# When the layer-0 experts' first loads count as ready: a change to the planner's costs in a two-layer mixture-of-experts kernel

## The chip, the cores and the metric

The kernel runs on one core of a Trainium2 chip. The metric is the device time of one execution in microseconds (us). The engines are named as in the profile: PE is TensorE (PEld its weight loads), DVE is VectorE, ACT is ScalarE, POOL is GpSimd and SP is SyncE, which issues most DMAs. L833 stands for line 833 of the kernel's source.

## The reference

Four sequences (B = 4) of 1024 tokens with 128 channels go through two layers. Each layer normalizes and modulates its input, adds a gated attention, normalizes and modulates again, and adds a gated mixture of experts. Cut to what matters here, the mixture of experts of layer 0:

```python
def _L0_ffn_ref(x, router_w, expert_w1, expert_b1, expert_w2, expert_b2):
    router_probs = softmax(einsum('bnc,ec->bne', x, router_w))
    expert_weights, expert_idx = top_k(router_probs, 2)
    expert_weights = expert_weights / (expert_weights.sum(-1, keepdims=True) + 1e-09)
    h = gelu(einsum('bnc,efc->bnef', x, expert_w1) + expert_b1, approximate=False)
    out_all = einsum('bnef,ecf->bnec', h, expert_w2) + expert_b2
    out_k = take_along_axis(out_all, expert_idx[..., None], axis=2)
    return (out_k * expert_weights[..., None]).sum(axis=2)

# layer 0
h = layernorm(x) * (1 + ca) + sa
x = x + ga * attention0(h)            # one head, causal, 128 channels
h = layernorm(x) * (1 + cb) + sb
x = x + gb * _L0_ffn_ref(h, ...)      # 8 experts, 512 hidden channels, 2 of 8 per token
# layer 1: the same frame; its attention has 16 heads of 8 channels, a second attention that keeps
# the 204 largest weights of each row, and a feed-forward part; its mixture of experts has a capacity
```

## The kernel before

All activations x are kept in on-chip memory, as [128 tokens, batch, 8 row tiles, 128 channels]. The work runs in these stages: the attention of layer 0 with the routing of its experts beside it; the experts of layer 0; the start of layer 1's attention; the long loop of layer 1's attention; the experts of layer 1.

**The experts of layer 0 go through memory outside the core.** For each batch b, `sent_out` normalizes x (the statistics on DVE, L482 and L486; the power -1/2 on POOL, L489; the shift on DVE, L492; the normalizing activations on ACT, L494), modulates the result on DVE (L746, L747), transposes it on PE (`ptf`, L755), computes the router's products (`pl`, L533), and then routes: a series of small DVE operations (`r_mx` to `into`, L545 to L630) with two matmuls `pp` (L595, L596) that count the tokens in front of each token. The result `into` says to which place of which expert's buffer each token's row goes. Sixteen indirect DMAs, issued by POOL (L785), write the rows to the buffer `sent`. Two batches share one buffer: batches 0 and 1 form the first half, batches 2 and 3 the second.

`worked_on(q)` then runs the experts on half q. It loads blocks of 384 and 256 rows of each expert from `sent` (`got`, L820, issued by SP), 16 blocks in all, and each load waits for all 32 indexed writes of its half. For every block PE transposes the rows (`ptg`, L833), DVE copies them out (`hs`, L835), PE makes the hidden rows (`ph`, L865) and ACT applies the activation (`hid`, L869), PE multiplies again (`py`, L850), DVE adds the bias (`y`, L855), and SP stores `y` to `done` (L856). Blocks follow each other in a pipeline: the transposes of block i stand in front of the hidden rows of block i-1 and the products of block i-2.

`fetched(b)` takes the results back: for each of the 8 row tiles POOL issues two indirect gathers from `done` (`ys`, L976); two row tiles later ACT scales one result (L988) and DVE adds the other, applies the gate and adds to x (L989, L990, L991). `begin(0)` starts layer 1's attention for batch 0: normalization, two elementwise operations on POOL (`h_`, L504), transposes on PE (L1257), projections, and two tensors `near` that are written out and loaded back by `project` in another layout (`kg`, `qg`, L1315). The first maxima of the attention (`pm` on PE, L1688; `mxh` on DVE, L1692) are the Part `early`.

**What sets the order.** Each engine executes its instructions in the order in which the program issues them. That order is made by a planner that runs while the program is written. Work is cut into pieces (generators that yield at the end of each piece), and a `Part` wraps a generator. Every yield names the costs of its piece as pairs of engine and microseconds; `spend` adds them to the planner's own clocks, `free["P"]`, `free["A"]`, `free["D"]` and `free["G"]` for PE, ACT, DVE and POOL, and returns the time at which the piece's result is there, which becomes the part's `ready`. An entry `("-", us)` is time on no engine. `fits` lets a piece go when its `ready` and the engines named in the yield's first string are not too far ahead of `free["P"]`. `drain` takes the first part of a list that fits; if none does, it moves `free["P"]` on by 0.2:

```python
            if e == "-":
                t += us
            else:
                ...
                t = free[e] = max(free[e], t) + us
            ...
            t += 0.06
```

These costs are the planner's; they only set the order. Two drains matter here:

```python
    drain([sends0[2], sends0[3], works0[0]])
    ...
                    drain([gets0[0], begins[0], projects[0, 0], early, gets0[1], works0[1]])
```

In the first, the routing of batches 2 and 3 (`sends0`) is planned beside the experts of the first half (`works0[0]`). In the second, the taking back of batches 0 and 1 (`gets0`), the start of layer 1 and its first maxima are planned beside the experts of the second half (`works0[1]`). After it the planner sets all its clocks to their maximum, and the attention loop places its side work by their differences.

Of the kernel before, what the change touches and what calls it, by code (L numbers as in the profile page):

```python
# [21 lines left out]
G = 4  # L22
# [26 lines left out]
def kernel(ctx: ExitStack, tc: tile.TileContext, a: dict, out: bass.AP):  # L49
# [456 lines left out]
    def rows_of(r, n=NT):  # L506
        return r.unsqueeze(1).to_broadcast([P, n, C])
# [291 lines left out]
    def behind(reads, writes, reason):  # L799
        for to in writes:  # L800
            tc.add_manual_dep(
                reads.ins, to.name,
                mybir.DependencyInfo(mybir.DependencyClass.Sync, mybir.DependencyReason.DATA),
                reason=reason,
            )

    def worked_on(q, w1, w2, b2r, fp):

        n = PLACES[0]
        units = [(e, i0, m) for e in range(E) for i0, m in RUNS]  # L810
        most = max(m for _, m in RUNS)
        gots, hss, hids = {}, {}, {}

        def at(u, t):
            e, i0, m = u
            return t[0][q][e * n + i0 * P : e * n + (i0 + m) * P].rearrange("(m p) c -> p m c", p=P)

        def load(u):
            gots[u] = fp.tile([P, most, C], F32, tag="got", bufs=4, name=f"got0{q}")
            got = nc.sync.dma_start(out=gots[u][:, : u[2]], in_=at(u, sent))  # L820
            behind(got, sent_by[0, q], "a place that any of them may have filled")

        load(units[0])
        load(units[1])
        yield "", ("-", 2.5)
        for i in range(len(units) + 2):
            if i < len(units):
                u = units[i]
                if i + 2 < len(units):
                    load(units[i + 2])  # L830
                pt = ps.tile([P, u[2], P], F32, tag="ms", name=f"ptg0{q}")
                for k in range(u[2]):
                    nc.tensor.transpose(pt[:, k, :], gots[u][:, k, :], ident)  # L833
                hss[u] = fp.tile([P, most * P], F32, tag="hs", name=f"hs0{q}")
                nc.vector.tensor_copy(hss[u][:, : u[2] * P], pt.rearrange("c m p -> c (m p)"))  # L835
                yield "A!", ("P", 0.25 * u[2]), ("D", 0.15 + u[2] * 0.14)
            if 1 <= i <= len(units):
                u = units[i - 1]
                hids[u] = fp.tile([P, NK, most * P], F32, tag="hid", name=f"hid0{q}")
                for k0 in range(0, NK, 2):  # L840
                    up(0, u[0], k0, hss[u][:, : u[2] * P], hids[u], AF.Gelu, w1)
                    us = u[2] * P / 512.0
                    yield "A!" if k0 == 0 else "!", ("P", 1.8 * us), ("A", 0.45 + 0.75 * us)
            if i >= 2:
                u = units[i - 2]
                e, _, m = u
                py = ps.tile([P, m, C], F32, tag="ms", name=f"py0{q}")
                for r in range(m):
                    for k in range(NK):
                        nc.tensor.matmul(  # L850
                            py[:, r, :], lhsT=hids[u][:, k, r * P : (r + 1) * P],
                            rhs=w2[:, e, k, :], start=(k == 0), stop=(k == NK - 1),
                        )
                y = fp.tile([P, most, C], F32, tag="y", name=f"y0{q}", bufs=3)
                nc.vector.tensor_tensor(y[:, :m], py, rows_of(b2r[:, e, :], m), ALU.add)  # L855
                nc.sync.dma_start(out=at(u, done), in_=y[:, :m])  # L856
                yield "!", ("P", 0.9 * m), ("D", 0.15 + 0.13 * m)
        yield "", ("-", 3.0)

    def up(l, e, k0, hs, hid, act, w1):  # L860

        n = hs.shape[1]
        ph = psb.tile([P, 2, 512], F32, tag="big", name=f"ph{l}{e}")
        for k in range(k0, k0 + 2):
            nc.tensor.matmul(  # L865
                ph[:, k - k0, :n], lhsT=w1[:, e, k * P : (k + 1) * P], rhs=hs, start=True, stop=True
            )
        for k in range(k0, k0 + 2):
            nc.scalar.activation(  # L869
                hid[:, k, :n], ph[:, k - k0, :n], act, bias=b1[l][:, e * NK + k : e * NK + k + 1]  # L870
            )
# [336 lines left out]
    for n in range(len(tiles) + 2):  # L1208
# [11 lines left out]
    drain(beside[len(begins0) + len(sends0) :] + sends0[:2])  # L1220
    works0 = [
        Part(worked_on(q, w1_0, w2_0, b2r0, f0), after=[sends0[2 * q + 1]])
        for q in range(2)
    ]
# [850 lines left out]
```

## Time and profile before

| | us |
|---|---|
| Median of 6 runs | 1937.03 |
| Lowest and highest of them | 1924.09, 1944.73 |
| The profiled execution | 1930.58 |
| Its span (first to last instruction) | 1928.8 |
| PE busy | 1747.8 (91% of the span) |
| DVE busy | 1279.6 (66%) |
| ACT busy | 1143.4 (59%) |
| POOL busy | 472.9 (25%) |

The mean granted clock of TensorE in the profiled execution was 0.949 of full speed. Matmuls are pipelined and their ends are modelled, so a busy PE is not a PE at its peak. In rows of the order of time, the first number is the start in us from the span's start, the second the time that the instruction (or the row of instructions of one kind) took; "x8" counts the instructions; the brackets at the end give how long the engine stood idle before and what released it. SPq is SyncE's queue of DMA issues; the time of such a row is the issue, not the transfer.

The stages that the change touches lie early in the span: the routing of layer 0 from about 70 us on, the experts' first half from 198 to 281 us, the second half with the start of layer 1 from 284 to 415 us. The loop of layer 1's attention starts at about 418 us.

### The profile page before, as it was taken

What the parts mean: (1) busy time and instruction counts of PE and PEld (TensorE: products, weight loads), DVE (VectorE), ACT (ScalarE), POOL (GpSimd) and SP (SyncE); (2) the same over time, 40 slices, a digit from 0 to 9 for tenths busy, and PEclk for the clock granted to TensorE, in tenths of its full rate; (3) what the DMA queues carried; (4) which work ended last, traced back from release to release, by engine and by line L of the source; (5) the groups of instructions that cost most, each with busy time, mean ns of one, the idle gap of its engine ahead of it and who ended that gap; (6) DMA issues with size and microseconds to landing.
All of it is one profiled execution on the core that took longest, in us unless ns stands there. A gap on an engine that the chain in (4) does not pass through costs nothing.

```text
span 1928.8 us, 33736 instructions
## 1 busy us (share of the span) xinstructions
PE 1747.8 (91%) x12781; PEld 882.0 (46%) x12781; DVE 1279.6 (66%) x3198; ACT 1143.4 (59%) x2317; POOL 472.9 (25%) x515
## 2 busy tenths in 40 slices
PE   6886899899999999998999999999999989999884
PEld 4655777552333434432344435234343423444674
DVE  5666414547877796577886676787776589882453
ACT  3533435246867765686773568778456887565543
POOL 1043356123011020103123110222410122431352
PEclk9988899999999999998998999999999989998998
DMA  8511233110000000000000000000000000002243
GB/s 299 173 34 42 84 95 87 50 44 25 11 18 12 7 2 7 1 7 6 23 12 9 7 1 7 1 17 18 18 5 5 5 6 5 19 1 73 75 116 94
DMA packets 82908, 73.24 MB, mean 38 GB/s; under 512 B 13560, under 2 KB 72521, under 8 KB 82737
## 3 DMA queue, kind: packets, MB, share of 16 engines
q1 hardware_dynamic: 74880, 57.06, 9.9%
q0 software_dynamic: 7424, 13.54, 2.4%
q8 instruction: 103, 1.69, 0.4%
q14 instruction: 69, 0.56, 0.1%
q10 hardware_dynamic: 432, 0.40, 0.1%
HBM read 35.92 MB, written 36.75 MB: 38 GB/s over the span
## 4 chain that ended last, share of the span: by engine, by line
PE 68%; DVE 13%; ACT 10%; issue 4%; DMA 3%; POOL 2%; SPq 0%; DVEq 0%; POOLq 0%; ACTq 0%
PE pw L1704 27%; PE pav L1726 12%; PE ph L865 4%; PE py L850 3%; PE po L1491 3%; DVE mxh L1692 3%; PE pm L1688 2%; ACT prT L1708 2%; DVE nm L1464 2%; ACT junk L1558 2%; ACT exq L1467 2%; PE pf L1805 2%; PE pk L1459 2%; PE ph L1792 1%; PE pscr L1131 1%
## 5 line engine op out<-in xcount | busy, mean ns | idle before, releaser
L1692 DVE TENSOR_REDUCE mxh<-pm 128x2 f32<-128x1024 f32 x512 | 620.5, 1220 | 212.0 <-PE pm L1688 209.3
L1704 PE MATMUL pw<-qa,kg 32*128 32x512 f32 x2048 | 708.5, 662 | 43.6 <-ACT prT L1708 32.4
L1708 ACT ACTIVATE prT<-pw 128x512 f32<-128x512 f32 x1024 | 556.5, 595 | 311.7 <-PE pm L1688 190.6
L1688 PE MATMUL pm<-kg,qg 32*128 32x512 f32 x2048 | 597.8, 663 | 3.3 <-DMA qg<-qk 2.2
L1704 PEld LDWEIGHTS pw<-qa,kg 32*128 32x128 f32 x2048 | 218.6, 189 | 311.1 <-issue 146.0
L1726 PE MATMUL pav<-prT,v_more 128*9 128x256 f32 x3584 | 288.6, 395 | 0.0
L1726 PEld LDWEIGHTS pav<-prT,v_more 128*9 128x9 f32 x3584 | 53.8, 89 | 356.2 <-issue 355.4
L869 ACT ACTIVATE hid<-ph,b 128x160 f32<-128x160 f32 (+2 forms) x256 | 100.1, 457 | 164.5 <-PE ph L865 164.2
L1558 ACT ACTIVATE junk<-exq,now 128x1024 bf16<-128x1024 f32 x160 | 184.7, 1155 | 9.2 <-DVE now L1585 8.5
L1688 PEld LDWEIGHTS pm<-kg,qg 32*128 32x128 f32 x2048 | 161.1, 189 | 13.5 <-DVE mxh L1692 6.0
L1641 POOL TENSOR_TENSOR exq<-exq,lfq 128x512 f32<-128x512 f32 x64 | 80.9, 1285 | 330.9 <-DVE lfq L1639 323.2
L865 PE MATMUL ph<-hs,w 128*128 128x160 f32 (+2 forms) x512 | 125.7, 388 | 16.2 <-DVE go L904 10.0
L865 PEld LDWEIGHTS ph<-hs,w 128*128 128x128 f32 x512 | 86.5, 201 | 40.1 <-DVE mxh L1692 7.9
L976 POOL DMA_INDIRECT ys<-done,outof x64 | 64.3, 1004 | 135.0 <-DMA qg<-qk 65.1
L785 POOL DMA_INDIRECT sent<-xns,into x64 | 62.7, 980 | 77.3 <-DVE into L625 30.9
L850 PEld LDWEIGHTS py<-w,hid 128*128 128x128 f32 x640 | 76.8, 195 | 7.1 <-issue 3.0
L850 PE MATMUL py<-w,hid 128*128 128x128 f32 x640 | 78.2, 279 | 0.0
L489 POOL TENSOR_TENSOR rs_l<-rs_l,mhalf 128x8 f32<-128x8 f32 (+1 forms) x10 | 14.0, 1404 | 225.8 <-DVE rs_l L488 225.8
L1491 PE MATMUL po<-sV,exT 128*128 128x129 f32 x512 | 65.6, 281 | 2.0 <-ACT exT L1487 1.1
L1491 PEld LDWEIGHTS po<-sV,exT 128*128 128x128 f32 x512 | 59.6, 191 | 15.7 <-issue 5.9
L1139 ACT ACTIVATE pr<-pscr,nm 128x128 f32<-128x128 f32 (+7 forms) x32 | 23.6, 739 | 69.3 <-DVE nm L1136 37.2
L1467 ACT ACTIVATE exq<-pk,nms 128x1024 f32<-128x1024 f32 x32 | 35.6, 1112 | 45.2 <-DVE nms L1466 45.0
(540 smaller groups left out, 2289.0 us busy)
## 6 DMA issues: line engine op xcount, KB each, us to landing
w<-in_w_dram SPq DMA_DIRECT2D x32, 256.0 KB
sent<-zero SPq DMA_DIRECT2D x2, 2560.0 KB
done<-zero SPq DMA_DIRECT2D x4, 1024.0 KB
qk<-near SPq DMA_DIRECT2D x8, 512.0 KB
ys<-done SPq DMA_DIRECT2D x16, 256.0 KB
got<-sent SPq DMA_DIRECT2D x16, 192.0 KB
done<-y SPq DMA_DIRECT2D x16, 192.0 KB
sent<-nowhere SPq DMA_DIRECT2D x4, 645.0 KB
```

The costliest lines, as they stand in the source:

```text
L850: nc.tensor.matmul(py[:, r, :], lhsT=hids[u][:, k, r * P : (r + 1) * P], rhs=w2[:, e, k, :], start=(k == 0), stop=(k == NK - 1),)
L865: nc.tensor.matmul(ph[:, k - k0, :n], lhsT=w1[:, e, k * P : (k + 1) * P], rhs=hs, start=True, stop=True)
L869: nc.scalar.activation(hid[:, k, :n], ph[:, k - k0, :n], act, bias=b1[l][:, e * NK + k : e * NK + k + 1])
L1467: nc.scalar.activation(ex, pk, AF.Exp, bias=nms, scale=rscale, accum_out=z)
L1491: nc.tensor.matmul(po, lhsT=exT[:, k, :], rhs=sVs[b % 2][:, k, :], start=(k == 0), stop=(k == NT - 1),)
L1558: nc.scalar.activation(junk, ex, AF.Sign, bias=now[:, i, 0:1], scale=-1.0, accum_out=now[:, i, 1:2],)
L1641: nc.gpsimd.tensor_tensor(ex[:, half(h)], ex[:, half(h)], lf[:, half(h)], ALU.subtract)
L1688: nc.tensor.matmul(pm[:, jj, :], lhsT=qg[js, t0 : t0 + P], rhs=kg[js, half(kh)], start=True, stop=True,)
L1692: nc.vector.tensor_reduce(mx[:, q, j0 : j0 + 2, kh], pm, AX.X, ALU.max)
L1704: nc.tensor.matmul(pw, lhsT=need(b, g, h)[1][js, k * P : (k + 1) * P], rhs=qas[b, g, h][js, :], start=True, stop=True,)
L1708: nc.scalar.activation(prs[b, g, h, k][:, j, :], pw, AF.Exp)
L1726: nc.tensor.matmul(to, lhsT=v, rhs=pr[:, j, cs], start=(k == 0), stop=((k, part) == (NT - 1, 1)),)
```

## The change

One yield of `worked_on` is changed. It stands behind the first two loads of a half, and names what the part waits for before its first transposes:

```diff
         load(units[0])
         load(units[1])
-        yield "", ("-", 2.5)
+        yield "", ("G", 0.0), ("-", 3.2)
         for i in range(len(units) + 2):
```

Before, the part counts as ready 2.5 us after time 0 of the planner, because a part that has not run yet starts from a `ready` of 0. After, the entry `("G", 0.0)` first takes the time to the planner's clock of POOL, `free["G"]`, to which the indexed writes that were issued so far have been added, and 3.2 us follow. Both halves of the experts go through this yield. No instruction of the chip is added, removed or altered by it, and no wait; the order of the instructions in the engines' queues can change.

## The prediction

> **What bounds the kernel now.** I read the page first, then the waits of the stretch that the edit touches, then that stretch in order of time.
>
> ```profile
> span 1928.8 us, 33736 instructions
> PE 1747.8 (91%) x12781; PEld 882.0 (46%) x12781; DVE 1279.6 (66%) x3198; ACT 1143.4 (59%) x2317; POOL 472.9 (25%) x515
> ```
>
> TensorE (PE) is busy 91% of the span, so a reordering can win only PE's idle stretches. The waits from 90 to 520 us give those of the layer-0 experts (groups by line: total, times, longest):
>
> ```profile
> PE ptg L833 <- DMA got<-sent: 19.1, 2, 15.3
> DVE hs L835 <- PE ptg L833: 19.7, 3, 13.0
> ```
>
> 19.1 us in two waits: the first expert transpose of each half waits for its loaded rows. In order of time, the first:
>
> ```profile
> 185.15 0.86 DVE L482 BATCH_NORM_STATS2 st_f<-x 128x6 f32<-128x128 f32 x4
> 193.21 0.97 POOL L785 DMA_INDIRECT sent<-xns,into  x1 [0.30 <-issue]
> 195.60 3.72 SPq L820 DMA_DIRECT2D got<-sent  x5
> 198.06 1.58 PE L833 MATMUL ptg<-ident,got 128*128 128x128 f32 x5 [15.28 <-DMA got<-sent]
> 200.01 0.18 DVE L566 TENSOR_SCALAR r_chosen<-r_left 128x64 f32<-128x64 f32 x1
> ```
>
> GpSimd (POOL) ends the 16 indexed writes of batch 1 at 194.18, SyncE issues the load at 195.60, PE starts at 198.06. VectorE (DVE) stood behind `hs` meanwhile and resumes batch 2's routing only at 200.01. The second:
>
> ```profile
> 284.04 1.08 POOL L976 DMA_INDIRECT ys<-done,outof  x1 [13.46 <-DMA done<-y]
> 284.74 1.30 PE L833 MATMUL ptg<-ident,got 128*128 128x128 f32 x5 [3.79 <-DMA got<-sent]
> 285.65 0.89 DVE L835 COPY hs<-ptg 128x384 f32<-128x384 f32 x2 [4.23 <-PE ptg L833]
> 286.26 4.66 PE L865 MATMUL ph<-hs,w 128*128 128x384 f32 x8 [0.22 <-DVE hs L835]
> ...
> 304.56 0.35 DVE L989 SCALAR_TENSOR_TENSOR ys<-ys,both 128x128 f32<-128x128 f32 x1 [1.75 <-DMA ys<-done,outof]
> 307.71 0.35 DVE L989 SCALAR_TENSOR_TENSOR ys<-ys,both 128x128 f32<-128x128 f32 x1 [2.15 <-ACT ys L988]
> 318.79 4.59 POOL L504 TENSOR_TENSOR h__3028<-h__3028,brow 128x512 f32<-128x512 f32 x4
> 322.30 0.66 PE L1257 MATMUL pt<-ident,h__3028 128*128 128x128 f32 x4 [2.44 <-POOL h__3028 L504]
> 347.97 1.35 SPq L1315 DMA_DIRECT2D kg<-qk  x4
> 352.81 1.55 PE L1688 MATMUL pm<-kg,qg 32*128 32x512 f32 x8 [2.21 <-DMA qg<-qk]
> ```
>
> Here `hs` of the second half goes at once; batch 0's gathers start at 284.04 and their last result is weighed (L989) at 307.71.
>
> **What the edit does to the order.** It adds and removes no instruction and no wait. It changes when the planner takes `worked_on` as ready, so only the order in the queues. I worked that order out from the costs in the source; no time below comes from them. When the first half's loads are issued, the planner's clocks stand at P 193.9, D 198.9, G 204.1. Ready was 0.06 + 2.5 = 2.6, at once. It becomes 204.1 + 0.06 + 3.2 + 0.06 = 207.4. Until then these go in front of the first transposes: the rest of batch 2's routing up to `into` (two matmuls `pp`), batch 3's last statistics, its power on POOL and its first four normalizing activations.
>
> The same function runs for the second half, which the edit's wording doesn't speak of. There P stands at 295.1 and the first piece of batch 0's gathers has just set G to 297.2, so ready is 297.2 + 3.3 = 300.5. Each gather piece is two gathers of 2.1, and a piece goes when G is at most P + 1.0. So gather pieces 0, 1 and 2 fit before P reaches 300.1; piece 2 holds the weighing of row tile 0 (one ACT, three DVE operations). It now stands ahead of the first `hs`, row tile 1 ahead of the second, row tile 2 ahead of `hs` of the third block, row tiles 6 and 7 ahead of the second activation of the third block's hidden rows. DVE and ACT run in order, so the experts now wait for gathers.
>
> **First half: -0.4 us.** The 15.28 us stays, since the writes that end at 194.18 and the load behind them are not moved. What moves into it is DVE work that no PE instruction waited for. Is it done in time? Batch 3's power now follows the writes on POOL: 194.6 to 196.25 (1.68 as at 213.45); its shift on DVE 196.6, six routing operations of 0.8 together (as from 211.79): 197.6, before 198.96, when `hs` could go. Cover 1.4 us; without it each us costs a us. From 204.75 on PE is busy without a break apart from a few tenths, so only `pp` (0.44 us, at 205.94) leaves the path. Bounds: -1.0, if the 0.54 us that batch 3's `pp` waits at 235.21 goes too, and +0.3, if the power slips by its whole length.
>
> **Second half, step by step.**
> 1. Row tile 0 needs the gathers at 284.04 and 285.43. A gather that DVE waited for was released 3.4 us after its start (301.16 to 304.56). So DVE has it at 288.8, three operations (0.35 + 0.29 + 0.29 with gaps: 1.1) to 289.9, `hs` 0.55, hidden matmuls at 290.2 instead of 286.26: +4.0. Bounds: the page's median from issue to landing is 2.6 (+3.1), the longest 4.8 (+5.4).
> 2. Row tile 7 still ends at 308.7: 16 gathers at 1.3. But the activation that frees a `big` buffer for the fourth block's second hidden pair is now behind it (307.7 to 308.75). PE reaches that pair at 305.5 and idles 3.3. The fifth block's PE work starts 7.3 late.
> 3. Batch 0's layer-1 normalization starts when row tile 7 is in x, as before. Its power starts 0.2 later. Then two gathers of batch 1 (2.6) now stand between the multiply and the add of `h_` on POOL (the 4.59 row was unbroken): PE's transposes at 322.30 go to 324.95, +2.65. PE reaches them at some 322.5, so step 2 is absorbed in this wait. But one block less is done by then (`ptg`, `ph`, `py`: 0.4 + 2.75 + 1.95 = 5.1): 7.75 behind.
> 4. The `kg`/`qg` loads come 4.84 us before the first `pm` (347.97 to 352.81), and follow SyncE's store of `y` of block 6. In front of `pm` stood 4.6 us of PE work after that block; now nothing. Counting PE's pieces by the rows from 338.05 on (1.3 + 1.1 + 1.3 + 1.9 + 1.8 + 1.7 + 0.3 + 1.8 + 2.7 = 13.9) from 340.65, block 6 ends at 354.5, the store is issued at 355.3, the loads at 355.75, `pm` goes at 360.6: +7.8, with an idle of 6.1 instead of 2.21.
> 5. Three pieces (2.9 us: `ptg`, `ph`) are still to do that were done before: 10.7 behind at the end of this stretch (before: 414.8).
>
> From there the planner sets all its clocks to their maximum, and the last pieces stand in the same relative order and distances; the order of the attention loop is the old one, only later. Nothing gives the loss back.
>
> **Sum.** -0.4 + 10.7 = +10.3 us. The profiled execution took 1930.58 (span 1928.8 and 1.8 around it): 1940.9. The runs shown have their median at 1937.03, 6.4 above it, so I name 1937.0 + 10.3 = 1947.3. Bounds of the sum: if the idle before `pm` is covered (-3.9) and gathers land by the median (-0.9), +5.5; with the longest landing (+1.4) and 4.8 us of half clock in the new idle, unabsorbed, +16.5.
>
> **The clock.** After the 3.16 us idle at 127.5, PE's granted clock was 0.51 from 130 to 140 and its rows lost 4.8 us; after 2.44 us at 319.9 sixteen 128-wide matmuls took 3.43 instead of 1.95. So I price the new 3.3 us idle as a cold start of 1.5 to 4.8, 2.4 of it absorbed by step 3. The Trainium skill (TensorE: Matmul & The Clock Gate, "What's actually happening") says that it takes about 3.4 us of idling to halve the clock. By that rule this idle is just too short and step 2 costs no cold start; the shorter idle above went cold all the same, and by the row up to 2.4 us would be added.
>
> **Rivals.**
> - *Neutral, or no move*: steps 3 and 4 hidden, or the planner's G below the writes' end so that nothing moves: 0 to +4, 1937 to 1941. For: PE is 91% busy and the tail is identical. Against: the in-order chain from the gathers to `hs`.
> - *Slower by over 1%*: the clock. If each of the three longer idles (before 290.2, 308.85, 360.6) costs the 4.8 us of the worst case, with what 284.74 (2.5) and 352.81 (2.1) already pay taken off: 14.4 - 4.6 = +9.8 on top, 1957.1. It decides once `ph` and `pm` run at half speed some 10 us after each. For: the 130 to 140 slice. Against: 286.26 recovered within 5 us.
> - *Faster*: both expert waits vanish, 15.28 + 3.79 = -19.1: 1918. For: they are PE's longest. Against: the writes and the last `done<-y` set them, and neither moves.
>
> **How the numbers follow.** Forecast 0.55, neutral 0.11, slower rival 0.27, faster 0.07. This kernel's runs tell about 1% (19.4 us) from no change. Faster by over 1%: most of the faster case, 0.05. Slower: the clock case and a small upper tail of the forecast, 0.30. Within 1%: 0.65. The range leaves out the faster case and the far end of the clock case, and allows for the spread of the runs' median: 1930 to 1964.
>
> **What would show it.** Right: `ptg` still at 198 after some 15 us; `r_chosen` near 186 and batch 2's writes from about 198 instead of 215; `ys` L989 before the first `hs` of the second half, with `hs` near 290; POOL's L504 broken by gathers; about 6 us of idle before the first `pm`; the attention loop some 10 us later. Wrong: a shorter first wait, `hs` before `ys`, or a main loop in another order.

## The result, and the profile after

The changed kernel takes 1952.33 us (median of 20 runs, 1932.23 to 1966.73), the kernel before 1932.9 (46 runs). The ratio is 1.0092, with a 95% interval of 1.0069 to 1.0114: some 17.8 us lost, between 13 and 22. It leaves out the five slowest of the 20 executions (1961.99 us and more); the two medians are 19.4 us apart. The forecast had +10.3. The profiled execution of the changed kernel took 1951.97 us.

From its page:

```profile
PE 1762.1 (90%) x12781; PEld 892.5 (46%) x12781; DVE 1281.9 (66%) x3198; ACT 1145.0 (59%) x2317; POOL 473.0 (24%) x515
```

TensorE executes the same 12781 matmuls, but is busy 14.3 us longer with them (1762.1 against 1747.8). Time in which a matmul waits is idle, not busy, in these rows, so part of the loss lies in slower matmuls: between the first `pm` and the first `pw` behind it TensorE is busy 68.07 us instead of 58.09. The waits from 90 to 520 us (total, times, longest):

```profile
PE ptg L833 <- DMA got<-sent: 12.2, 2, 8.3
...
DVE hs L835 <- PE ptg L833: 5.7, 3, 2.6
...
PE pm L1688 <- DMA qg<-qk: 6.5, 1, 6.5
...
PE ph L865 <- DVE hs L835: 5.2, 2, 5.0
```

The expert waits have gone from 19.1 to 12.2 us (the rest of the first stands before `pp` now), and the time is longer all the same. Two other waits have grown: the first `pm` waits 6.5 us for its loads (2.2 before), and `ph` waits 5.0 us for `hs` (0.2 before). The first half in order of time (start, length, instruction, idle before it and its releaser):

```profile
187.87 0.18 DVE L566 TENSOR_SCALAR r_chosen<-r_left 128x64 f32<-128x64 f32 x1
188.19 0.66 PE L595 MATMUL pp<-r_chosen,earlier 128*128 128x64 f32 x2 [3.46 <-DVE r_chosen L566]
...
191.21 0.69 PE L596 MATMUL pp<-r_before,ones 128*128 128x64 f32 x2 [2.36 <-DVE r_before L589]
...
195.16 0.97 POOL L785 DMA_INDIRECT sent<-xns,into  x1 [0.30 <-issue]
197.55 3.91 SPq L820 DMA_DIRECT2D got<-sent  x5
...
199.33 1.04 POOL L785 DMA_INDIRECT sent<-xns,into  x1 [1.50 <-ACT xns L494]
200.20 1.30 PE L833 MATMUL ptg<-ident,got 128*128 128x128 f32 x5 [8.30 <-DMA got<-sent]
```

Two `pp` now cut the old 15.28 us wait into 3.46, 2.36 and 8.30: 14.1 us of idle and the two `pp`. The transposes still start 5.0 us after the start of batch 1's last write (195.16 to 200.20; 4.85 before). Batch 2's writes begin at 199.33 instead of 215.32, and nothing on TensorE had been waiting for them. The second half:

```profile
285.56 1.08 POOL L976 DMA_INDIRECT ys<-done,outof  x1 [27.77 <-DMA done<-y]
...
286.33 1.30 PE L833 MATMUL ptg<-ident,got 128*128 128x128 f32 x5 [3.86 <-DMA got<-sent]
...
291.09 0.35 DVE L989 SCALAR_TENSOR_TENSOR ys<-ys,both 128x128 f32<-128x128 f32 x1 [8.16 <-DMA ys<-done,outof]
...
292.01 0.55 DVE L835 COPY hs<-ptg 128x384 f32<-128x384 f32 x1
...
292.62 5.49 PE L865 MATMUL ph<-hs,w 128*128 128x384 f32 x8 [4.98 <-DVE hs L835]
...
307.91 0.35 DVE L989 SCALAR_TENSOR_TENSOR ys<-ys,both 128x128 f32<-128x128 f32 x1 [0.68 <-DMA ys<-done,outof]
...
319.00 2.32 POOL L504 TENSOR_TENSOR h__2981<-h__2981,brow 128x512 f32<-128x512 f32 x2
...
323.94 2.32 POOL L504 TENSOR_TENSOR h__2981<-h__2981,brow 128x512 f32<-128x512 f32 x2
...
325.18 0.66 PE L1257 MATMUL pt<-ident,h__2981 128*128 128x128 f32 x4 [1.97 <-POOL h__2981 L504]
...
361.64 2.58 PE L1688 MATMUL pm<-kg,qg 32*128 32x512 f32 x8 [6.52 <-DMA qg<-qk]
...
368.12 3.35 PE L1688 MATMUL pm<-kg,qg 32*128 32x512 f32 x8
...
377.60 3.48 PE L850 MATMUL py<-w,hid 128*128 128x128 f32 x16
...
381.02 1.14 PE L1688 MATMUL pm<-kg,qg 32*128 32x512 f32 x8
```

`hs` stands behind the weighing of row tile 0 (L989), the add and the multiply of L504 are apart, and `pm` starts at 361.64: the chain that the prediction had drawn. The last lines show what it had not: eight matmuls of `pm` take 2.58 us at 361.64 and 3.35 at 368.12, and eight of the same form take 1.14 at 381.02. The granted clock, which this text calls half or cold at 0.50 and warm at 1.00, stands behind the four busy times in each row of the windows (window, its length, PE, PEld, DVE, ACT, POOL, clock, DMA share, GB/s):

```profile
358.00:360.00 2.00, 0.00 (x0) 0.00 (x0) 0.00 (x0) 0.00 (x0) 0.00 (x0) 1.00 0.27 88
360.00:362.00 2.00, 0.35 (x2) 0.39 (x3) 0.00 (x0) 0.00 (x0) 0.00 (x0) 0.54 0.31 78
362.00:364.00 2.00, 2.00 (x8) 0.65 (x7) 0.02 (x1) 0.00 (x0) 0.00 (x0) 0.50 0.00 0
...
380.00:382.00 2.00, 2.00 (x15) 1.21 (x14) 0.42 (x1) 0.00 (x0) 0.00 (x0) 0.84 0.00 0
```

The clock is at 0.50 from about 360.2 to 380.6 (0.54 and 0.84 are mixtures of 0.50 and 1.00 within 2 us), with TensorE busy nearly throughout. In the kernel before, between `pm` and `pw`, it was at 0.50 from 354.8 to 358.2 only.

Three distances locate the loss. The first `ptg` of the first half to that of the second: 86.68 us before, 86.13 after (-0.55). From there to the first `pm`: 68.07 and 75.31 (+7.24). From there to the first `pw` behind it, with which the attention loop begins: 65.36 and 74.52 (+9.16). (Some expectations call it the last `pw`; the same instruction is meant.) Together +15.9 us, inside the interval of the measured loss. The rest of the two profiles' difference lies ahead of the first `ptg` (2.1 us) and behind `pw` (3.4 us), where VectorE, ScalarE and GpSimd have the same instructions in the same order in both kernels.

### The profile page after: what moved, and what is told of

Its sections match the earlier page's. It is cut to its first block, busy times and chain, and to the rows that moved or that the text cites. A ratio compares the mean times of both kernels' runs of the same rounds, so it can differ in the third digit from the quotient of the medians.

```text
span 1950.2 us, 33742 instructions
## 1 busy us (share of the span) xinstructions
PE 1762.1 (90%) x12781; PEld 892.5 (46%) x12781; DVE 1281.9 (66%) x3198; ACT 1145.0 (59%) x2317; POOL 473.0 (24%) x515
## 4 chain that ended last, share of the span: by engine, by line
PE 64%; DVE 10%; ACT 8%; issue 3%; DMA 2%; POOL 2%; SPq 0%; POOLq 0%; DVEq 0%; ACTq 0%
PE pw L1704 26%; PE pav L1726 11%; PE ph L865 4%; PE po L1491 3%; PE py L850 3%; DVE mxh L1692 3%; PE pm L1688 3%; ACT prT L1708 2%; DVE nm L1464 2%; ACT exq L1467 2%; PE pf L1805 2%; PE pk L1459 2%; ACT junk L1558 2%; PE ph L1792 1%; PE ptm L1665 1%
## 5 line engine op out<-in xcount | busy, mean ns | idle before, releaser
L865 PE MATMUL ph<-hs,w 128*128 128x160 f32 (+2 forms) x512 | 130.1, 397 | 20.1 <-DVE go L904 9.1
L855 DVE TENSOR_TENSOR y<-py,b2r 128x384 f32<-128x384 f32 (+1 forms) x32 | 15.7, 490 | 74.6 <-PE py L850 74.6
```

The lines of the kernel that those rows point to most:

```text
L865: nc.tensor.matmul(ph[:, k - k0, :n], lhsT=w1[:, e, k * P : (k + 1) * P], rhs=hs, start=True, stop=True)
```

## The experiments

My theory after this result: (a) the first half is neutral; (b) the second half's new place in the queues costs the 7 us before `pm`; (c) the longer idle before `pm` turns the clock down and it stays down for 20 us, which is the part that the sum had lacked. The rivals: the first half's reordering costs something later, or the long `pm` rows come from loads and VectorE and not from the clock.

Beside the first four kernels (the two halves alone, the short filler, the loads named) the kernel before took 1999.32 us itself. In the profiles of these four, and in no other, engines pause with a releaser that the trace calls remote, most of all between 120 and 340 us (13.4 us before a `pp` on TensorE, up to 14.8 on other engines). I therefore read these four by their distances from the second half's first `ptg` on, besides their ratios.

**The first half alone.**

```diff
-        yield "", ("G", 0.0), ("-", 3.2)
+        yield ("", ("-", 2.5)) if q else ("", ("G", 0.0), ("-", 3.2))
```

> The changed yield only for the first half (batches 0 and 1); the second half keeps the old one. Theory (the whole loss comes from the second half, where gathers now stand ahead of the first hs): PE starts the second half about 0.4 us earlier against the start of the first half, hs of the second half goes at once again, the distance from the first expert transpose of the second half to the first pw is the old one (133.4 us); ratio to before 0.999 to 1.001. Rival (the routing moved in front of the first half costs something itself): the distance from the first to the second half's first transposes grows over the old 86.7 us, and the ratio is 1.004 or more.

Measured: 2004.94 us, ratio 1.0037 (1.0003 to 1.0070). From the second half's first `ptg` to the first `pw` 136.1 us, against 133.43; some 2 to 3 us of that are gaps within one `py` block that the trace puts down to issue. From the first `pm` to `pw` 65.5, as before. The ratio lies above what the theory allowed, so the kernel was run once more, beside others, when the kernel before took 1930.58.

> The new waiting time for the first half alone, the old one for the second: the kernel of e1_first_half once more, beside the others of this call, since its ratio of 1.0037 was above what its own stretch could explain. Theory: from the first expert transpose of the first half to that of the second 86.1 (before 86.7), from there to the last pw 133.4 as before; ratio 0.998 to 1.001. Rival (moving batches 2 and 3's routing ahead costs something later that the sum did not see): ratio 1.003 or more, with the stretch that carries it visible between these marks.

Measured: 1929.06 us, ratio 0.9999 (0.9974 to 1.0023); 85.84 us from the first `ptg` to the second half's, and 132.06 from there to the first `pw`. Its second half in order of time:

```profile
288.04 1.33 PE L833 MATMUL ptg<-ident,got 128*128 128x128 f32 x5 [3.78 <-DMA got<-sent]
...
288.95 0.89 DVE L835 COPY hs<-ptg 128x384 f32<-128x384 f32 x2 [4.23 <-PE ptg L833]
...
289.56 4.89 PE L865 MATMUL ph<-hs,w 128*128 128x384 f32 x8 [0.19 <-DVE hs L835]
```

Both `hs` go at once and `ph` waits 0.19 us for them, not 4.98. The first half is neutral; the 1.0037 did not come back. The loss has to be in the second half.

This profile shows one thing more. The old idle before `pm` is there, and the clock does not fall behind it:

```profile
356.35 1.53 PE L1688 MATMUL pm<-kg,qg 32*128 32x512 f32 x8 [2.27 <-DMA qg<-qk]
357.81 2.05 PE L850 MATMUL py<-w,hid 128*128 128x128 f32 x16
```

In the kernel before the same sixteen `py` took 3.34 us, behind 2.21 us of idle. In each of the thirteen profiles the changes of the granted clock stand a whole number of steps of 3.41 us apart. Two such steps of the kernel before, then two of this one:

```profile
351.40:354.81 3.41, 2.00 (x12) 1.27 (x13) 1.21 (x6) 0.29 (x1) 1.20 (x2) 1.00 0.20 50
354.81:358.22 3.41, 3.41 (x18) 3.04 (x20) 2.10 (x3) 0.00 (x0) 0.00 (x0) 0.50 0.00 0
```

```profile
351.76:355.17 3.41, 2.32 (x8) 1.04 (x6) 1.48 (x7) 2.34 (x5) 2.75 (x2) 1.00 0.49 119
355.17:358.58 3.41, 2.23 (x14) 1.50 (x15) 1.18 (x5) 0.00 (x0) 0.99 (x1) 1.00 0.17 44
```

In the first, 1.41 us of one step are idle, and the next step has the half clock; in the second the idle is split, 1.09 and 1.18 us, and the clock stays. So an idle of 2.2 us costs a cold start in some executions and not in others. Idle time alone does not decide: in the changed kernel the step from 353.33 to 356.75 had 1.63 us of it, and the clock fell only behind the next one, which was idle throughout. What in a step does decide stays open.

**The second half alone.**

```diff
-        yield "", ("G", 0.0), ("-", 3.2)
+        yield ("", ("G", 0.0), ("-", 3.2)) if q else ("", ("-", 2.5))
```

> The changed yield only for the second half. Theory: the whole loss is here: the first hs of the second half waits for row tile 0 of the gathers, an idle of 6 us before the first pm, the distance from the second half's first transposes to the first pw near 149.8 us as in the changed kernel instead of 133.4; ratio 1.007 to 1.011. Rival (the two halves only lose together, because the earlier routing lets the writes of batch 3 end earlier): the distance stays below 140, ratio under 1.004.

Measured: 2019.04 us, ratio 1.0088 (1.0052 to 1.0123), the whole loss of the change. From the second half's first `ptg` to `pw` 154.6 us, above the 149.8 of the changed kernel; one `py` block (332.4 to 340.3 us), broken by gaps that the trace puts down to issue, takes some 6 us longer than elsewhere. From `pm` to `pw` 74.3. The matmuls behind the idle have the same lengths as in the changed kernel:

```profile
394.57 2.57 PE L1688 MATMUL pm<-kg,qg 32*128 32x512 f32 x8 [6.44 <-DMA qg<-qk]
...
401.06 3.35 PE L1688 MATMUL pm<-kg,qg 32*128 32x512 f32 x8
```

**A short filler before `pm`.** 20 transposes of the identity into a tile that nobody reads, in the changed kernel:

```diff
             def prologue():
 
+                if not general:
+                    warm = ps.tile([P, 4, P], F32, tag="ms", name="warm")
+                    for k in range(20):
+                        nc.tensor.transpose(warm[:, k % 4, :], ident, ident)
                 for _ in range(20):
```

> The changed kernel with 20 transposes of the identity, which nobody reads, put on PE straight before the first pm, into the 6.5 us in which it waits for kg and qg; the order of everything else is that of the changed kernel. Theory (after that idle PE stays at half clock for some 20 us, and this is the 6 us that the prediction's sum lacks): pm still starts at the same distance from the last product before it (some 9.4 us from that product's start), but pm, ph and py in the 20 us behind it take 1.14, 1.56 and 2.05 us instead of 2.58, 2.93 and 3.48, and the stretch from the first pm to the first pw shrinks from 74.5 to about 68 us; ratio 0.003 below that of the changed kernel. Rival (the lacking 6 us are waits for DVE's maxima and the shared buffers in the new order): the stretch stays at 73 us or more though the rows are short.

Measured: 2024.18 us, ratio 1.0127 (1.0085 to 1.0169). The 20 transposes took only 2.35 us and left 4.36 us of idle; the `pm` rows took 2.57, 3.35 and 3.29 as before, and `pm` to `pw` 74.5. The dose was too small, and the run decides nothing.

**The loads named.** In the changed kernel the prologue gets a first piece that tells the planner when `kg` and `qg` come:

```diff
             def prologue():
 
+                if not general:
+                    yield "", ("D", 0.0), ("-", 7.0)
                 for _ in range(20):
```

> The changed kernel, and the planner is told that the first maxima are ready only 7 us after the loads of kg and qg are issued (a first piece of the prologue without instructions), so that pieces of the experts stand in front of the first pm. Theory (idle 6.5 us before the first pm and the half clock behind it make 10 of the 16 us that the second half lost): idle before the first pm under 1 us, no half clock behind it, the stretch from the second half's first transposes to the first pw 138 to 141 us instead of 149.8; ratio 1.002 to 1.006. Rival (PE is held by DVE's maxima in this stretch, which now start later): the stretch is 146 us or more and the ratio within 0.002 of the changed kernel's.

Measured: 2012.2 us, ratio 1.0076 (1.0045 to 1.0106); 142.05 us from the second half's first `ptg` to `pw`, somewhat above the 138 to 141 expected and far from 146, and 60.6 from `pm` to `pw`. Pieces of two more blocks of experts stand in front of `pm` now:

```profile
397.40 2.00 PE L1688 MATMUL pm<-kg,qg 32*128 32x512 f32 x8
399.33 2.94 PE L850 MATMUL py<-w,hid 128*128 128x128 f32 x24
402.20 1.14 PE L1688 MATMUL pm<-kg,qg 32*128 32x512 f32 x8
```

No idle, and no row at half speed. It removes the idle and the slow clock together, so it does not separate them yet. The ratio stayed above the 1.006 expected and within 0.002 of the changed kernel's 1.0092, as its rival had it: by the whole time the gain is not shown.

**A longer filler.** 52 transposes instead of 20.

> The changed kernel with 52 transposes of the identity into a tile that nobody reads, ahead of the first pm. Twenty such transposes took 2.35 us in the run e3_warm and left 4.36 us of idle; 52 should take some 6.1 and leave under 1 us. Theory (the 6 us that the sum lacked are the half clock that follows the idle): the first pm rows come at the usual 1.14 us each instead of 2.58, 3.35 and 3.29, and the distance from the first pm to the last pw falls from 74.5 to 66-68 us; the whole from the second half's first transpose to pw from 149.8-155 to 142-147, ratio against the kernel before 1.002 to 1.008. Rival (these rows are long because the loads and VectorE hold them, not the clock): the rows stay above 2.5 us, or become short while pm to pw stays 73 or more.

Measured: 1944.82 us, ratio 1.0071 (1.0046 to 1.0095). From `pm` to `pw` 75.3 us: read by its own expectation, the theory had lost.

```profile
353.31 5.84 PE L1909 MATMUL warm<-ident 128*128 128x128 f32 x52
361.29 2.52 PE L1688 MATMUL pm<-kg,qg 32*128 32x512 f32 x8 [2.14 <-DMA qg<-qk]
```

But the filler had again not filled the idle: the first `pm` came 8.0 us after it began, and 2.14 us stayed; the next eight `pm` took 3.35 us as before. The granted clock in this kernel stayed at 1.00 through the filler and fell to 0.50 at about 362, when `pm` already ran. Either 2.1 us of idle were enough, or `pm` itself does it. The next kernel tells these apart.

**No idle at all.** 80 transposes, 8.9 us by the row above (0.112 us each).

> The changed kernel with 80 transposes of the identity into a tile that nobody reads, ahead of the first pm: 80 of 0.112 us, 9.0 us together, as long as the 8.4 us from the end of py to the first pm in e5_warm_long, where 52 left 2.14 us idle and the pm rows stayed long. Theory (it is the idle ahead of pm that lets the clock fall, and 2.1 us of it are enough): with no idle left the granted clock stays at 1.00 behind the fillers, the pm rows come at 1.14 to 2.0 us, and from the first pm to the last pw it takes 60 to 67 us instead of 74.5; ratio 1.002 to 1.007. Rival (the clock falls because of the pm rows themselves, 32 partitions wide, mixed with ph, whatever stood ahead): granted clock 0.50 for some 20 us again, 73 us or more.

Measured:

```profile
349.12 8.90 PE L1909 MATMUL warm<-ident 128*128 128x128 f32 x80
357.95 1.14 PE L1688 MATMUL pm<-kg,qg 32*128 32x512 f32 x8
...
361.91 2.40 PE L1688 MATMUL pm<-kg,qg 32*128 32x512 f32 x8
```

The granted clock is 1.00 from 350 to beyond 380, and `pm` to `pw` takes 67.3 us instead of 74.5, just above the 60 to 67 expected and far from the rival's 73. The loads and VectorE's work are the same as in the changed kernel. So the long rows are the clock, and the idle brings it down. Of the 7.2 us, 1.5 go for `pm` itself, which comes later behind the fillers: from the second half's first `ptg` to `pw` it is 144.14 instead of 149.83. No gain in the whole time stands beside this: 1952.39 us, ratio 1.0107 (1.0071 to 1.0143) from 4 runs, above the 1.002 to 1.007 expected. The part after `pw` took 1527.5 us in this profile and 1514.0 in that of the changed kernel (last section); I take the missing gain for that spread, but did not show it.

**The idle left, an unbroken run behind it.** 40 unread transposes after the second piece of the prologue, in the changed kernel:

```diff
-                for _ in range(20):
+                for j in range(20):
                     next(ahead)
+                    if j == 1 and not general:
+                        warm = ps.tile([P, 4, P], F32, tag="ms", name="warm")
+                        for k in range(40):
+                            nc.tensor.transpose(warm[:, k % 4, :], ident, ident)
```

> The changed kernel with 40 unread transposes of the identity behind the first two pieces of pm, so the idle ahead of pm is left as it is, but an unbroken run of 128-partition matmuls follows at once, as the block of py does in the kernel before. Theory (the half clock ends only behind such a run, which the changed kernel has 15 us later): the fillers take 5 to 8 us, the clock is 1.00 some 4 to 6 us after their start, the second and third group of pm rows take 1.14 to 2.4 instead of 3.35 and 3.29, and from the first pm to the last pw it takes 68 to 73 us although 40 transposes are added. Rival (the half clock lasts some 20 us whatever runs): granted 0.50 until 380, 79 us or more.

Measured, in order of time and in windows:

```profile
353.83 2.58 PE L1688 MATMUL pm<-kg,qg 32*128 32x512 f32 x8 [6.50 <-DMA qg<-qk]
356.34 5.77 PE L1911 MATMUL warm<-ident 128*128 128x128 f32 x40
...
363.55 2.40 PE L1688 MATMUL pm<-kg,qg 32*128 32x512 f32 x8
```

```profile
356.00:358.00 2.00, 2.00 (x11) 1.66 (x9) 1.80 (x2) 0.00 (x0) 0.00 (x0) 0.50 0.03 8
358.00:360.00 2.00, 2.00 (x17) 2.00 (x16) 0.56 (x1) 0.00 (x0) 0.00 (x0) 0.80 0.00 0
360.00:362.00 2.00, 2.00 (x21) 2.00 (x20) 0.00 (x0) 0.00 (x0) 0.00 (x0) 1.00 0.00 0
```

The same 6.50 us of idle and the same cold first `pm`, but the clock is back at about 358.8, 2.5 us after the fillers began (4 to 6 were expected); in the changed kernel it came back 19 us after `pm` began. From `pm` to `pw` 73.07 us, at the upper end of the 68 to 73 expected; without the 5.77 of fillers it is 67.3 again. How long the half clock lasts is set by what runs behind the idle. The whole time was 1951.73 us (median of 5, of which one, 3765.69 us, stands unexplained and is not in the ratio), ratio 1.0110 (1.0072 to 1.0148): no gain. In the stretch the fillers cost nearly what they bring back.

**Attempts at a faster version.** First the kernel before, with only the loads named (the edit above, with 2.5 for 7.0):

> The kernel before, and in it only a first piece of the prologue that names the time of its loads, so that one py block and one ptg (2.4 us) stand ahead of the first pm. Theory: the 2.21 us of idle and the short cold stretch behind it go; from the second half's first transpose to the last pw 129 to 131.5 instead of 133.4, pm rows 1.14 instead of 1.55 and 2.12; ratio 0.997 to 0.9995. Rival (the idle only moves behind the pieces that were moved, or the pieces are missed later): 133 or more, ratio 1.000 or more.

Measured: 1934.14 us, ratio 1.0011 (0.9982 to 1.0039); 134.4 us from the second half's first `ptg` to `pw`. A miss, and the rival's way:

```profile
353.28 1.31 PE L865 MATMUL ph<-hs,w 128*128 128x256 f32 x4 [2.22 <-DVE mxh L1692]
354.52 3.07 PE L1688 MATMUL pm<-kg,qg 32*128 32x512 f32 x8
```

`pm` comes without idle, but the idle of 2.2 us moved behind it, to `ph`, which waits for VectorE's maximum; the clock falls all the same (3.07 for eight `pm`). Then the same with the new waiting time in the first half:

> The new waiting time for the first half alone, together with the named loads of e7_only_loads_named: the version that should beat both kernels if the first half's gain is real. Theory: the two effects add up, -0.4 to -0.6 before the second half and -2 to -4 after it: ratio 0.9965 to 0.9995, and no slower than e7_only_loads_named. Rival (the first half's reordering costs what e1_first_half seemed to show): ratio 1.001 or more, and above e7_only_loads_named by 0.3%.

Measured: 1934.09 us, ratio 1.0031 (1.0005 to 1.0056), 131.47 us from the second half's first `ptg` to `pw`. By the whole time slightly slower, if anything, though its stretch is the shorter one. The idle before `ph` is there too (2.17 us), but here the clock stays at 1.00: of the 2.9 us between the two stretches, which have the same instructions in the same order, 2.8 lie behind `pm`, at a cold start that came in one profile and not in the other. Last, the first half alone with 24 transposes before `pm`, so that the kernel's old idle of 2.2 us is covered:

> The new waiting time for the first half alone, and 24 unread transposes of the identity (2.7 us) ahead of the first pm, which cover the 2.2 us of idle that the kernel before has there. Theory: no half clock at 353 to 358 any more; pm, py, pm at 1.14 to 1.3, 2.05 and 1.14 instead of 1.55, 3.34 and 1.44, less 0.5 for the fillers that outlast the loads; from the second half's first transpose to the last pw 130 to 131.5 instead of 132.1 to 133.4, and 85.8 to 86.2 before it; ratio 0.997 to 1.000, so the fastest kernel of the study if anything is. Rival (the cold stretch was not worth what its rows lost, something else holds the loop): 132 or more.

Measured: 1927.23 us, ratio 0.9985 (0.9963 to 1.0007).

```profile
348.89 2.78 PE L1909 MATMUL warm<-ident 128*128 128x128 f32 x24
352.13 1.54 PE L1688 MATMUL pm<-kg,qg 32*128 32x512 f32 x8 [0.45 <-DMA qg<-qk]
353.60 2.05 PE L850 MATMUL py<-w,hid 128*128 128x128 f32 x16
```

`py` takes 2.05 us instead of 3.34, no window falls below 1.00 there, and the stretch takes 131.5 us. But `pm` to `pw` takes 63.75 us with these fillers and took 63.75 in the first half alone without them, where `py` took 2.05 as well: what the fillers add is not shown. The kernel has the lowest ratio of the study, but the interval includes 1: by the whole time it can't be called faster.

## Why the prediction was right in kind and short in size

- *First half, -0.4*: neutral, as forecast; so small a gain can't be told from the spread. -0.55 in the two profiles, but the kernel with only the loads named, whose first half is the old one, has 85.71 us here, less than the changed kernel's 86.13. Ratio 0.9999 for this half alone. The wait is still the indexed writes and the load behind them; only the `pp` moved into it.
- *Step 1, `ph` +4.0*: right. Measured from the second half's first `ptg`, `ph` came at 6.29 instead of 1.52 us, +4.8, because the data of row tile 0 were at VectorE 5.5 us after the first gather's start (285.56 to 291.09), where I had taken 4.8. (With 40, 52 and 80 fillers, whose order is the same, it came at 5.08, 5.23 and 6.48: +3.6 to +5.0.)
- *Step 2, an idle of 3.3 us for a `big` buffer*: did not happen in this profile. The fourth block's `ph` ran unbroken from 307.95 to 309.84; PE reached the second pair at some 308.8, and the activation that frees its buffer, behind row tile 7 as foreseen, had ended at 308.15. (The one wait for an activation in this stretch, 1.11 us at 319.41, is in the sixth block.) The order is as forecast: with 40 and with 52 fillers, where `ph` of the first block had come 1.1 to 1.2 us earlier, the same pair waits 1.39 and 0.77 us. I had put row tile 7 at its old place against the first gather. It came 1.4 us earlier relative to `ptg` (21.58 us after it instead of 22.97): ScalarE got its gather 2.8 us after that gather's start (303.97 to 306.80), in the kernel before 4.8 us after it (302.46 to 307.28), the longest landing there. In the profiles without remote pauses this takes 2.6 to 2.9 us in the new order and 3.1 to 4.8 in the old one; why, no run shows.
- *Step 3, transposes of `h_` +2.65*: the two gathers between the multiply and the add are there, but the transposes are only 1.3 us later. The 1.4 us of step 2 are the difference.
- *Step 4, `pm` +7.8 with an idle of 6.1*: right, +7.24 and 6.52. It hit partly because two errors met: the chain to `pm` began some 1.6 us earlier than counted, which is step 3's error, but its PE pieces took 14.4 us instead of 13.9 (a half of a long `ph` takes 1.5, not 1.3) and the idle was 0.4 longer.
- *Step 5, 2.9 us more to `pw`*: the term that was mis-sized. It measured 9.16. Without the half clock the changed kernel takes 67.3 us here (80 fillers; with the 40 behind the first `pm` taken off it is the same, though that `pm` was still cold), and the old second half takes 63.7 without its own short cold stretch (415.87 - 352.13, and the same in the first half alone). So 3.6 of it are the pieces that I had put at 2.9; 74.5 - 67.3 = 7.2 are the half clock, and the 1.6 that the kernel before already paid (65.4 - 63.7) go off: 3.6 + 7.2 - 1.6 = 9.2.
- *The clock*: priced at the wrong idle. I gave a cold start to step 2, whose idle did not come, and put step 4's 6.1 us into the sum as time alone. The "slower" rival had the right mechanism, but at three idles with 4.8 us each. It came at the last of them with 7.2, 5.6 net; at the first, `ph` lost 0.8 more than before (5.49 against 4.66, inside the +7.24), and the second idle was not there. Of its signs, `pm` at half speed some 10 us after the idle was there.
- *The time*: +10.3 forecast, +15.9 in the two profiles, about +17.8 in the runs. The named time, 1947.3, is only 5.0 under the measured one because the kernel before was put at 1937.0 from 6 runs and took 1932.9 in 46: that is luck. The forecast's class, slower by less than 1%, held by a small margin: 1.0092, with an interval that goes past 1.01. That the rest of the loss beyond +15.9 is spread is likely, not shown.

The Trainium skill (TensorE: Matmul & The Clock Gate, "What's actually happening") says that about 3.4 us of idle turn the clock down and about 3.4 us of sustained work turn it up, counted in a window that runs freely. The traces agree with the window: the steps of 3.41 us above. For the way up they agree where the work is an unbroken run: 2.5 us after the 40 fillers began, and 3.0 us after `py` began in the changed kernel. The 16 us of `pm` and `ph` ahead of that `py`, with TensorE marked busy nearly throughout, did not turn it up. For the way down, idles of 2.06 to 2.22 us were enough in four profiles (the kernel before, the first half alone at its first run, the 52 fillers, only the loads named) and 2.17 and 2.27 us were not in two others; part of the measured fall came after work had begun again. No run here moved one idle against the steps on purpose.

## What to carry to other kernels

When a planner's cost of one piece changes, look at every call of that function: here one half was neutral and the harm lay wholly in the other, where gathers came to stand ahead of the experts in VectorE's in-order queue. Price a longer wait of TensorE as the wait plus what runs behind it at half clock, and look at what that is: an unbroken run of matmuls of 128 partitions ended it in 2.5 to 3.9 us, a mixture of short groups did not end it in 16. An idle that is filled by reordering may only move to the next in-order engine. And compare a short cold start over more than one profile: the same order of work showed it in one and not in the next.

## What the runs showed of the hardware that was not expected

- The mixture of `pm` (32 partitions) and `ph` behind the idle kept, in these profiles, the clock that it found. With `pm` starting warm it ran at 1.00 (358 to 368 us in the kernel with 80 fillers, groups of 2.4 us); starting cold, the same instructions ran at 0.50 for the 16 us up to the first `py` block. TensorE was marked busy at least 1.58 of every 2 us of that, once `pm` had begun.
- The part after `pw` has the same 10766 matmuls in all kernels, yet took between 1508.8 us (PE busy 1399.7) and 1528.2 (busy 1420.5) in the nine profiles without remote pauses, with mean granted clocks of 0.96 and 0.94. Half-clock stretches that come and go between executions go along with most of the spread of this kernel's times: over the 33 executions of the kernel before that stand beside the 52 fillers, the correlation of time and mean granted clock is -0.96 (1945.68 us at 0.941, 1921.41 at 0.956). A change of a few us is hidden by it in 4 to 12 executions.
- The kernel before took 1999.32 us in the median beside the first four experiments and 1930.58 and 1933.91 beside the others; pauses marked remote stand in the profiles of these four only. What caused them stays open.
